# Seven products of blocks for the queries and the attention output of a macaron transformer block

## The chip, the cores and the metric

The kernel runs on one core of one Trainium2 chip. A core has five engines, each with its own queue of instructions that it works off in order: TensorE (matmuls; PE in the profile, its weight loads PEld), VectorE (DVE), ScalarE (ACT), GpSimd (POOL) and SyncE (SP), whose queue here issues every transfer between the memory outside the core and its own memory (SBUF). Matmuls write into PSUM, eight banks of 512 float32 per partition. Engines wait for each other by semaphores only. The metric is the device time of one execution in microseconds (us); the median of three runs counts.

## The reference

Eight sequences of 512 tokens with 512 features go through half a feed-forward, attention, and half a feed-forward again, everything in float32:

```python
x = x + 0.5 * ffn(layernorm(x))
x = x + attn(layernorm(x))
x = x + 0.5 * ffn(layernorm(x))

def ffn(x):
    h = silu(x @ w_gate) * (x @ w_up)            # 512 -> 2048
    return keep_two_largest_of_four(h) @ w_down  # by magnitude; 2048 -> 512

def attn(x):
    Q, K, V = x @ W_q, x @ W_k, x @ W_v          # 16 query heads, 4 key/value heads of 32
    Qr, Kr = rope(Q), rope(tile(K))              # rotation of neighbouring pairs
    weights = softmax(Qr @ Kr.T / sqrt(32))
    return (weights @ tile(V)) @ W_o
```

## The kernel before

The program is one long list of instructions, written by generators that a planner lets take turns. Sixteen feed-forwards ("blocks": eight sequences, two each, in a fixed order) are the main line. Everything else, the layernorm that gets a block's input ready and the eight attentions, are "sides": each is cut into steps, each step has a due place, counted in groups of matmuls of the main line (about 3.45 us each), and a step is written down when its due place has come and its inputs are there by the planner's own clock (`at`, three counters for TensorE, VectorE and ScalarE), or when it is three groups late. An attention runs over about 70 groups, and the next one begins where it ends.

VectorE's work stands in three waiting lists: `soon` (urgent), `later` (put off) and `for_later`. `fill`, called after each product, writes down as much of it as VectorE can finish by the time TensorE is done; last come the steps that zero two of four hidden values. `ensure` forces entries out.

The feed-forward already multiplies blocks with seven products in place of eight (the scheme of Strassen and Winograd): inputs and weights are cut into 2x2 quarters, sums of quarters are multiplied, and the products are put together. `woven` does it for gate and up: seven products of four matmuls, each 128x128 by 128x256, into three banks (x, v and z). Between the products VectorE and ScalarE copy or add a bank into its place. `product` (L561) does the same for the down projection with eight matmuls a product. The quarters of w_gu are loaded 16 ahead (`load_quarters`, L115 and L117), those of w_down three ahead. The sums of weights are made once: of w_gu in the first block by VectorE (`combine_gu`), of w_down by GpSimd (`combine_down`, two sides in the first block, into a big tile of the slot "wa").

An attention (`attention(b)`) has these steps:

- the layernorm (`layernorm_t`, tag "xa"): four row tiles of 128 tokens are loaded (L287), normalised and transposed into xT, with the features on the partitions; meanwhile the weights and the rotation tables cs are loaded (L798);
- five projections (`projected`, L809): K and four chunks of Q, each four matmuls of 128x128 by 128x512 into one of the same three banks. VectorE rotates each with four instructions: a shuffle of neighbours from the bank, a multiplication by the cosine from the bank, one by the sine, and a sum;
- V (L834): 16 matmuls 128 wide;
- scores and softmax per chunk of four heads, with matmuls on 32 rows each (L853, L886), maxima by VectorE, exponentials by ScalarE, sums by VectorE, weighted values (L902) and the division. The scores fill the four banks of the slot "sc";
- the output (L988): four products, each four matmuls 128x128 by 128x512, one per 128 tokens; VectorE adds each to the residual xt, and SP stores it (L996).

The slots: "p" holds two big tiles, used in turn by cs, xT, total and p; "wa" one, for wqkv and then wo; "xa" four row tiles, for xn and then xt. A tile is written only when all readers of the tile before it in the place are done.

The query projection is this:

```python
ps = Bank([P, S], "proj")
for k in range(ND):
    nc.tensor.matmul(out=ps.tile, lhsT=wa[:, k, col : col + P], rhs=xT[:, k, :], start=(k == 0), stop=(k == ND - 1))
```

Of the kernel before, what the change touches and what calls it, by code (L numbers as in the profile page):

```python
# [11 lines left out]
FP = mybir.dt.float32  # L12
# [6 lines left out]
P = 128  # L19
# [7 lines left out]
def macaron_block(  # L27
# [29 lines left out]
    wdp = ctx.enter_context(tc.tile_pool(name="wdp", bufs=3))  # L57
    sp = ctx.enter_context(tc.tile_pool(name="sp", bufs=1))
    wap = ctx.enter_context(tc.tile_pool(name="wap", bufs=1))
    qkvp = ctx.enter_context(tc.tile_pool(name="qkvp", bufs=1))  # L60
    pp = ctx.enter_context(tc.tile_pool(name="pp", bufs=2))
    xnp = ctx.enter_context(tc.tile_pool(name="xnp", bufs=4))
# [69 lines left out]
    z = const.tile([P, NT, N_KV, HD], BF, name="z")  # L132
    nc.vector.memset(z, 0.0)
    identb = const.tile([P, P], BF, name="identb")

# [13 lines left out]
    def multiplied(us, tiles=False):  # L151

        takes("pe", us + (SWITCH if tiles != tiled[0] else 0.0))
        tiled[0] = tiles
# [26 lines left out]
    def later(us, does, ready=None, queue=put_off):  # L181
        queue.append(Later(us, does, pe_heard() if ready is None else ready, queue))
        return queue[-1]
# [32 lines left out]
    w_slots = Slots(work, "w", 2)  # L216
    row_slots = Slots(cp, "row", 2)
    corner_slots = Slots(cp, "corner", 2)
    wa_slots = Slots(wap, "wa", 1)
    sc_slots = Slots(ps_sc, "sc", 1)  # L220
    acc_slots = Slots(ps_acc, "acc", 1)

# [56 lines left out]
    def layernorm_t(got, tag, src=None, xb=None):  # L279

        xn = []
        for t in range(NT):
            xn.append(xnp.tile([P, D], FP, tag=tag, name="xn"))
            if xb is None:
                nc.sync.dma_start(out=xn[t], in_=src[t * P : (t + 1) * P, :])  # L287
        mv = small.tile([P, NT, 2], FP, tag="mv", name="mv")
# [38 lines left out]
        def sums():  # L327

            xT = got["xT"]
            (b11, b12), (b21, b22) = ([xT[:, 2 * i : 2 * i + 2, j * HALF : (j + 1) * HALF] for j in range(2)] for i in range(2))  # L330
            got["sums"] = ts = tp.tile([P, 4, 2, HALF], FP, tag="ts", name="ts")
            got["made"] = [
                later(0.62, partial(nc.vector.tensor_tensor, ts[:, i], a, b, ALU.subtract), at["act"])
                for i, a, b in ((0, b12, b11), (1, b22, ts[:, 0]), (2, b22, b12), (3, b21, ts[:, 1]))
            ]

        if xb is None:
# [18 lines left out]
            for t in range(NT):  # L356
                turn(t)
                yield by_scalar if t < NT - 1 else now
            if tag == "xf":
                sums()  # L360
        else:

            function(AF.Sqrt)
# [16 lines left out]
    def fill(slack=HEARD):  # L380

        while True:
            steps = thin["next"]
            for queue in (urgent, put_off, for_later):
                if queue and queue[0].fits(slack):
                    queue[0].run()
                    break
            else:
                if not steps:
                    return  # L390
                ready = steps[1] if isinstance(steps[1], float) else steps[1]()
                if max(at["dve"], ready) + steps[0] > at["pe"] + slack:
                    return
                step()
# [101 lines left out]
    def combine_down(g):  # L496

        for c in range(2 * g, 2 * g + 2):
            raw = p_slots.tile([P, 4, D], FP, "raw")
            for r in range(4):  # L500
                nc.sync.dma_start(out=raw[:, r], in_=w_down[c][:, r])
                there = at["pe"] + 5.0
                yield now if r < 3 else lambda: there
            quarter = {f"{i + 1}{j + 1}": raw[:, i::2, j * HD2 : (j + 1) * HD2] for i in range(2) for j in range(2)}
            sums = wa_slots.tile([P, 6, 2, HD2], FP, "sums")

            for i, name in enumerate(SUMS):
                of = quarter[name[3:]] if name[3:] in quarter else sums[:, int(name[4:]) - 1]
                nc.gpsimd.tensor_tensor(sums[:, i], quarter[name[:2]], of, ALU.subtract)
                nc.sync.dma_start(out=combined[g, name][:, c % 2 * 2 : c % 2 * 2 + 2, :], in_=sums[:, i])  # L510
            yield now
        done_down.add(g)

# [266 lines left out]

    heads = [slice(kv * HD, (kv + 1) * HD) for kv in range(N_KV)]

    def attention(b):
        ensure(written[b, 0])
        wa = wa_slots.tile([P, ND, D + 2 * KV], FP, "wqkv")
        cs = p_slots.tile([P, 4, S], FP, "cs")
        loads = deque()
        for src, col in ((w_k, D), (w_v, D + KV)):
            loads.append((wa[:, :, col : col + KV], src.rearrange("(c p) n -> p c n", p=P)))
        for i in range(2):  # L790
            loads.append((cs[:, i], rope[i]))
        for k in range(ND):
            loads.append((wa[:, k, :D], w_q[k * P : (k + 1) * P, :]))
        got = {}
        for ready in layernorm_t(got, "xa", tokens[b][1]):
            if loads:
                dst, src = loads.popleft()
                nc.sync.dma_start(out=dst, in_=src)  # L798
            yield ready
        xT = got["xT"]  # L800
        qT = qkvp.tile([P, ND, S], FP, tag="qT", name="qT")
        kT = qkvp.tile([P, S], FP, tag="kT", name="kT")
        v = qkvp.tile([P, NT, KV], FP, tag="v", name="v")

        def projected(dst, col, scale):

            ps = Bank([P, S], "proj")
            for k in range(ND):
                nc.tensor.matmul(  # L809
                    out=ps.tile, lhsT=wa[:, k, col : col + P], rhs=xT[:, k, :], start=(k == 0), stop=(k == ND - 1)  # L810
                )
            multiplied(3.43)
            fill()
            sw = w_slots.tile([P, S], FP, "sw")
            soon(0.65, partial(nc.vector.stream_shuffle, sw, ps.tile, SWAP))
            read = soon(
                0.62, partial(nc.vector.scalar_tensor_tensor, dst, ps.tile, scale, cs[:, 0, :], ALU.mult, ALU.mult)
            )
            ps.free([read])
            soon(0.65, partial(nc.vector.scalar_tensor_tensor, sw, sw, scale, cs[:, 1, :], ALU.mult, ALU.mult))  # L820
            made = soon(0.65, partial(nc.vector.tensor_tensor, dst, dst, sw, ALU.add))
            return [p_slots.used(w_slots.used(made), 1)]

        of_k = projected(kT, D, 1.0)
        yield now
        of_q = []
        for c in range(ND):
            of_q.append(projected(qT[:, c, :], c * P, 1.0 / math.sqrt(HD)))
            yield now
        ensure(of_q[-1])  # L830
        vps = Bank([P, NT, KV], "vps")
        for t in range(NT):
            for k in range(ND):
                nc.tensor.matmul(  # L834
                    out=vps.tile[:, t, :],
                    lhsT=xT[:, k, t * P : (t + 1) * P],
                    rhs=wa[:, k, D + KV : D + 2 * KV],
                    start=(k == 0),
                    stop=(k == ND - 1),
                )  # L840
# [1 line left out]
        fill()  # L842
        nc.scalar.copy(v, vps.tile)
        vps.free(end=takes("act", 0.6, pe_heard()))
        wo = wa_slots.tile([P, ND, D + 2 * KV], FP, "wo")
        yield partial(when, of_k + of_q[0])

        def scores(c, t, nm):

# [82 lines left out]


        nm = maxima()
        ensure(of_k + of_q[0])
        for t in range(NT):
            found = scores(0, t, nm)
            nc.sync.dma_start(out=wo[:, t, :D], in_=w_o[t * P : (t + 1) * P, :])
            yield partial(when, found)
        pieces = in_pieces(nm)  # L940
        yield partial(when, pieces)
# [34 lines left out]
        waits(end)  # L976
        weighted(NT - 1, ops, p)
        out_of = divided(c, ops, sums)
        xts = []
        for t in range(NT):  # L980
            xts.append(xnp.tile([P, D], FP, tag="xa", name="xt"))
            nc.sync.dma_start(out=xts[t], in_=tokens[b][1][t * P : (t + 1) * P, :])
        yield partial(when, out_of)
        waits(ensure(out_of))
        for t, xt in enumerate(xts):
            y = Bank([P, D], "y")
            for k in range(ND):
                nc.tensor.matmul(  # L988
                    out=y.tile, lhsT=qT[:, k, t * P : (t + 1) * P], rhs=wo[:, k, :D], start=(k == 0), stop=(k == ND - 1)
                )  # L990
            multiplied(3.43)
            fill()

            def add(t=t, xt=xt, y=y):
                nc.vector.tensor_tensor(xt, y.tile, xt, ALU.add)
                nc.sync.dma_start(out=tokens[b][2][t * P : (t + 1) * P, :], in_=xt)  # L996

            made = [soon(0.62, add)]
            y.free(made)
            if t == NT - 1:  # L1000
                ensure(made)
            yield now

# [2 lines left out]
    WIDTH = 7 * NCH + 7 * NCH // 2  # L1008
    NORM = 5 + 2 * NT

    WEIGHTS = [0.5] * (NORM + ND + 2) + [0.7] * (NT + 1) + [0.9, 0.9] * NT
    WEIGHTS += ([0.9, 1.2] + [0.9, 0.9] * (NT - 1)) * (ND - 2) + [1.5] + [1.3] * (NT - 1) + [1.5] + [0.5] * NT
    ATTENTION = len(WEIGHTS)

    def place(b, i):
        return WIDTH * blocks.index((b, i))


    sides = [(10, 19, 10, partial(combine_down, 0), None, None), (22, 34, 10, partial(combine_down, 1), None, None)]
    for b, i in blocks[1:]:  # L1020
        stage = partial(layernorm_t, normed[b, i], "xf", tokens[b][2 * i])
        sides.append((place(b, i) - 15, place(b, i) - 2, NORM, stage, ("attention", b) if i else None, None))
# [106 lines left out]
```

## Time and profile before

| what | us |
|---|---|
| median of 3 runs | 3211.94 (3211.62 to 3216.32) |
| the profiled execution, whole | 3210.11 |
| its span, first to last instruction | 3208.2 |
| TensorE busy | 3176.9 |
| VectorE busy | 2189.8 |
| ScalarE busy | 1195.8 |
| GpSimd busy | 507.2 |
| of TensorE's time along the chain that ended last: projections L809 | 4.3% |
| output products L988 | 3.4% |

Busy time is the time in which an engine has at least one instruction at work. Matmuls overlap at their ends, and a float32 matmul stands as two records; so the length of a matmul row is longer than its share of the time, and the distance from one start to the next is the price. A wait is idle time of an engine with the instruction that ended it. The engines' shares are averages over stages, and only an engine that others wait for costs time.

### The profile page before, as it was taken

The numbers are of one execution on the slowest core, as the hardware profiler recorded it, in microseconds if no ns is written. First come the engines' busy times: TensorE is split into PE (matmuls) and PEld (weight loads), VectorE is DVE, ScalarE is ACT, GpSimd is POOL, SyncE is SP. The second block draws the span as 40 slices with busy tenths as digits, with TensorE's granted clock in tenths as the row PEclk, the third lists the DMA queues.
The fourth block names the chain that finished last, engine by engine and source line by source line (L and its number), as shares of the span: only waits on it lengthen the run. The fifth ranks groups of instructions, "written<-read, shape, count | busy, mean of one in ns | idle before, by whom it ended". The sixth has DMA issues, their size and how long they took to land.

```text
span 3208.2 us, 43276 instructions
## 1 busy us (share of the span) xinstructions
PE 3176.9 (99%) x15880; PEld 2322.4 (72%) x15880; DVE 2189.8 (68%) x4718; ACT 1195.8 (37%) x1683; POOL 507.2 (16%) x822
## 2 busy tenths in 40 slices
PE   8999999999999999999999999999999999999999
PEld 6887767767677677766776677766776677666886
DVE  7756876587657785678657865777567765776554
ACT  2222454145522553245314542255324441454220
POOL 2322102110021111101211102111120121111110
PEclk9999999999999999999999999999999999999999
DMA  7763344434443436334444344443633444434441
GB/s 236 240 216 99 122 158 144 142 128 126 156 158 126 132 119 210 96 121 152 145 143 131 122 153 159 133 132 112 210 99 119 161 141 142 131 122 154 154 165 53
DMA packets 263731, 462.15 MB, mean 144 GB/s; under 512 B 25952, under 2 KB 81760, under 8 KB 263264
## 3 DMA queue, kind: packets, MB, share of 16 engines
q1 hardware_dynamic: 263520, 459.38, 44.2%
q8 instruction: 127, 2.08, 0.3%
q14 instruction: 84, 0.69, 0.1%
HBM read 421.53 MB, written 37.75 MB: 143 GB/s over the span
## 4 chain that ended last, share of the span: by engine, by line
PE 96%; DVE 2%; DMA 1%; ACT 1%; POOL 0%; issue 0%; SPq 0%; POOLq 0%; DVEq 0%
PE x L636 27%; PE v L636 13%; PE x L561 13%; PE z L636 7%; PE v L561 6%; PE proj L809 4%; PE st L886 4%; PE sc L853 4%; PE ops L902 4%; PE y L988 3%; PE z L561 3%; PE tr L263 1%; PE gu L611 1%; PE den L918 1%; PE vps L834 1%; PE st L891 1%
## 5 line engine op out<-in xcount | busy, mean ns | idle before, releaser
L636 PE MATMUL x<-ts,w 128*128 128x256 f32 x3000 | 717.3, 382 | 1.4 <-DVE corner L650 1.4
L636 PEld LDWEIGHTS x<-ts,w 128*128 128x128 f32 x3000 | 561.7, 190 | 137.9 <-issue 44.3
L452 POOL TENSOR_TENSOR e<-h 128x512 f32<-128x512 f32 x62 | 79.3, 1279 | 2232.5 <-DVE h L446 1892.9
L165 DVE TENSOR_REDUCE nm<-sc 128x1 f32<-128x512 f32 x512 | 321.1, 683 | 95.3 <-PE sc L853 94.0
L561 PE MATMUL x<-wd,h 128*128 128x256 f32 x1488 | 339.9, 382 | 0.0
L165 DVE TENSOR_TENSOR total<-total,p 128x512 f32<-128x512 f32 x384 | 273.8, 749 | 81.1 <-ACT p L894 81.1
L561 PEld LDWEIGHTS x<-wd,h 128*128 128x128 f32 x1488 | 280.2, 190 | 62.5 <-issue 19.3
L894 ACT ACTIVATE p<-st 128x2048 f32<-128x2048 f32 x96 | 179.7, 1872 | 291.1 <-PE st L891 279.8
L255 ACT ACT_TABLE_LOAD x215 | 275.8, 1283 | 4.5 <-PEq L1118 0.7
L243 ACT COPY row<-x 128x512 f32<-128x512 f32 x207 | 121.2, 585 | 393.0 <-PE x L636 392.9
L685 ACT ACTIVATE h<-x 128x256 f32<-128x256 f32 x125 | 47.6, 381 | 555.2 <-PE x L636 543.3
L636 PE MATMUL v<-ts,w 128*128 128x256 f32 x1000 | 239.0, 382 | 2.4 <-ACT xT L324 2.4
L636 PE MATMUL x<-xT,w 128*128 128x256 f32 x1000 | 239.4, 382 | 1.8 <-ACT xT L324 1.8
L636 PE MATMUL v<-xT,w 128*128 128x256 f32 x1000 | 238.5, 382 | 1.5 <-DVE corner L245 1.5
L636 PE MATMUL z<-xT,w 128*128 128x256 f32 x1000 | 238.9, 382 | 0.0
L561 PE MATMUL v<-wd,e 128*128 128x256 f32 x992 | 228.2, 382 | 7.1 <-POOL e L452 4.0
L561 PEld LDWEIGHTS v<-wd,e 128*128 128x128 f32 x992 | 186.2, 190 | 52.6 <-issue 13.3
L636 PEld LDWEIGHTS x<-xT,w 128*128 128x128 f32 x1000 | 186.9, 190 | 49.2 <-issue 20.4
L636 PEld LDWEIGHTS v<-ts,w 128*128 128x128 f32 x1000 | 187.3, 190 | 46.2 <-issue 16.2
L636 PEld LDWEIGHTS z<-xT,w 128*128 128x128 f32 x1000 | 187.1, 190 | 45.6 <-issue 19.3
L636 PEld LDWEIGHTS v<-xT,w 128*128 128x128 f32 x1000 | 187.7, 190 | 42.8 <-issue 10.1
L407 ACT ACTIVATE a<-h 128x1024 f32<-128x1024 f32 x128 | 134.9, 1054 | 186.0 <-DVE m L425 106.8
(115 smaller groups left out, 4448.8 us busy)
## 6 DMA issues: line engine op xcount, KB each, us to landing
w<-gu SPq DMA_DIRECT2D x472, 256.0 KB, 3.4
w<-in_w_gu SPq DMA_DIRECT2D x394, 256.0 KB, 3.4
wd<-wd SPq DMA_DIRECT2D x124, 512.0 KB, 5.4
wd<-in_w_down SPq DMA_DIRECT2D x186, 256.0 KB, 3.6
x<-x SPq DMA_DIRECT2D x64, 256.0 KB, 2.6
xn<-x SPq DMA_DIRECT2D x64, 256.0 KB, 5.0
x<-in_x SPq DMA_DIRECT2D x32, 256.0 KB, 3.7
gu<-w SPq DMA_DIRECT2D x32, 256.0 KB, 2.9
```

What stands on the lines that cost most here:

```text
L165: self.does()
L243: nc.scalar.copy(dst, src)
L255: nc.scalar.activation(dummy[:, 1:2], dummy[:, 0:1], f)
L407: nc.scalar.activation(a, h[:, :, half * HALF : (half + 1) * HALF], AF.Abs)
L561: nc.tensor.matmul(out=y.tile[:, t, :], lhsT=part[:, t * P : (t + 1) * P], rhs=operands[i][:, n, :], start=(first and t == 0 and n == 0), ...
L636: nc.tensor.matmul(out=bank.tile[:, m, :], lhsT=lhs[:, m, k, :], rhs=rhs[:, k, :], start=(first and m == 0 and k == 0), stop=(k == 1), ski ...
L809: nc.tensor.matmul(out=ps.tile, lhsT=wa[:, k, col : col + P], rhs=xT[:, k, :], start=(k == 0), stop=(k == ND - 1))
L853: nc.tensor.matmul(out=sc[:, kv, :], lhsT=qT[rows, c, t * P : (t + 1) * P], rhs=kT[rows, :], start=True, stop=True)
L886: nc.tensor.matmul(out=st[:, kv, :], lhsT=kT[rows, t * P : (t + 1) * P], rhs=qT[rows, c, :], start=True, stop=False)
L894: nc.scalar.activation(p, st, AF.Exp)
L902: nc.tensor.matmul(out=ops[rows, :], lhsT=v[:, t, rows], rhs=p[:, kv, :], start=(t == 0), stop=(t == NT - 1))
L988: nc.tensor.matmul(out=y.tile, lhsT=qT[:, k, t * P : (t + 1) * P], rhs=wo[:, k, :D], start=(k == 0), stop=(k == ND - 1))
```

## The change

The four query projections become seven products of four matmuls 128x128 by 128x256, and so do the four output products. They go to three of the four banks of the scores' slot (bank order 0, 1, 0, 1, 0, 2, 0), one product a step, with other work between. The factors:

- queries: sums of quarters of w_q, made once, by sums of quarters of the tokens, made per attention by VectorE in a tile of the "p" slot; the first three products are copied to their places in qT, the next three added there and rotated, and the last is rotated from the bank;
- output: quarters and sums of the heads' outputs (four sums by VectorE per attention) by quarters and sums of w_o; all seven products are added to the residual.

The sums of w_q and w_o are made by VectorE in the second block (`combine_qo`) and stored to memory outside. All quarters are loaded through four small tiles ("waq"), each next one when a product is written down. The rotation tables are loaded once (`load_cs`). The sums of w_down, by GpSimd as before, also use the four small tiles. xn and xt of an attention become one tile each of four rows. The attention has more steps, so their spacing changes. w_q and w_o are laid out by quarters before the launch. The diff, cut:

```diff
+    waq = ctx.enter_context(tc.tile_pool(name="waq", bufs=4))
...
+    cs = const.tile([P, 2, S], FP, name="cs")
...
-    wa_slots = Slots(wap, "wa", 1)
...
-        xn = []
+        if tag == "xf":
+            xn = [xnp.tile([P, D], FP, tag=tag, name="xn") for _ in range(NT)]
+        else:
+            xa = xnp.tile([P, NT, D], FP, tag=tag, name="xn", bufs=1)
+            xn = [xa[:, t, :] for t in range(NT)]
...
+            if tag == "xf":
+                got["sums"] = ts = tp.tile([P, 4, 2, HALF], FP, tag="ts", name="ts")
+            else:
+                got["sums"] = ts = p_slots.tile([P, 4, 2, HALF], FP, "ts")
             got["made"] = [
-                later(0.62, partial(nc.vector.tensor_tensor, ts[:, i], a, b, ALU.subtract), at["act"])
+                (later if tag == "xf" else soon)(
+                    0.62, partial(nc.vector.tensor_tensor, ts[:, i], a, b, ALU.subtract), at["act"]
+                )
...
-            sums = wa_slots.tile([P, 6, 2, HD2], FP, "sums")
+            sums = []
+            for name in SUMS:
+                sums.append(waq.tile([P, 2, HD2], FP, tag="waq", name="sum"))
...
+    def combine_qo():
+        for which, how in (("q", Q_SUMS), ("o", O_SUMS)):
+            both = [p_slots.tile([P, 4, 2, HALF], FP, "both") for _ in range(2)]
+            w = [both[q // 4][:, q % 4] for q in range(8)]
+            for q in range(4):
+                nc.sync.dma_start(out=w[q].rearrange("p a b -> p (a b)"), in_=flat(qo_raw[which][q]))
+                there = at["pe"] + 5.0
+                yield now if q < 3 else lambda: there
+            for to, a, b, op in how:
+                made = later(0.65, partial(nc.vector.tensor_tensor, w[to], w[a], w[b], op), queue=for_later)
+            yield partial(when, [made])
+            ensure([made])
+            nc.sync.dma_start(out=qo_sums[which], in_=both[1])
+            yield now
+
+    def load_qo(which, q):
+        w = waq.tile([P, 4 * P], FP, tag="waq", name="waq")
+        src = flat(qo_raw[which][q]) if q <= Q21 else flat(qo_sums[which][:, q - S1])
+        nc.sync.dma_start(out=w, in_=src)
+        return w
...
+        def seven(lhs, rhs, take):
+            sc = sc_slots.tile([P, N_KV, 2, HALF], FP, "seven")
+            waits(sc_slots.ready)
+            order = 0, 1, 0, 1, 0, 2, 0
+            taken = {bank: [] for bank in order}
+            for i, bank in enumerate(order):
+                waits(ensure(taken[bank]))
+                w = weights.popleft()
+                for m in range(2):
+                    for k in range(2):
+                        nc.tensor.matmul(
+                            out=sc[:, bank, m, :],
+                            lhsT=lhs(w, i, m, k),
+                            rhs=rhs(w, i, k),
+                            start=(i in (0, 1, 5) and m == 0 and k == 0),
+                            stop=(k == 1),
+                            skip_group_check=True,
+                        )
+                multiplied(1.73)
+                load_next()
+                fill()
+                taken[bank] = take(i, sc[:, bank])
+                for entry in taken[bank]:
+                    sc_slots.used(entry)
+                yield partial(when, taken[order[i + 1]] if i < 6 else [])
...
-        for c in range(ND):
-            of_q.append(projected(qT[:, c, :], c * P, 1.0 / math.sqrt(HD)))
-            yield now
...
+        def take_query(i, bank):
...
+            if i < 3:
+                return [Done(copied((left, corner, right)[i], bank))]
+            if i == 6:
+                return rotate(below, 0, bank)
+            to, j = ((right, 1), (corner, 1), (left, 0))[i - 3]
+            entry = soon(0.62, partial(nc.vector.tensor_tensor, to, bank, to, ALU.add))
+            rotate(to, j)
+            return [entry]
+
+        yield from seven(
+            lambda w, i, m, k: w[:, (2 * m + k) * P : (2 * m + k + 1) * P],
+            lambda w, i, k: tokens_of[i][:, k, :],
+            take_query,
+        )
+        yield partial(when, of_k + of_q)
...
-        xts = []
+        xt = xnp.tile([P, NT, D], FP, tag="xa", name="xt", bufs=1)
         for t in range(NT):
-            xts.append(xnp.tile([P, D], FP, tag="xa", name="xt"))
-            nc.sync.dma_start(out=xts[t], in_=tokens[b][1][t * P : (t + 1) * P, :])
+            nc.sync.dma_start(out=xt[:, t, :], in_=tokens[b][1][t * P : (t + 1) * P, :])
...
+        combined_heads = p_slots.tile([P, 4, 2, HALF], FP, "sums")
...
+        def take_output(i, bank):
+            def add(to):
+                nc.vector.tensor_tensor(to, bank, to, ALU.add)
+                if i >= 5:
+                    for t in (0, 1) if i == 5 else (2, 3):
+                        nc.sync.dma_start(out=tokens[b][2][t * P : (t + 1) * P, :], in_=xt[:, t, :])
+
+            made = [soon(0.62, partial(add, (left, corner, right, right, corner, left, below)[i]))]
+            if i == 6:
+                ensure(made)
+            return made
...
-    WEIGHTS = [0.5] * (NORM + ND + 2) + [0.7] * (NT + 1) + [0.9, 0.9] * NT
-    WEIGHTS += ([0.9, 1.2] + [0.9, 0.9] * (NT - 1)) * (ND - 2) + [1.5] + [1.3] * (NT - 1) + [1.5] + [0.5] * NT
+    WEIGHTS = [0.5] * (NORM + 2 + 7 + 1) + [0.7] * (NT + 1) + [0.9, 0.9] * NT
+    WEIGHTS += ([0.9, 1.2] + [0.9, 0.9] * (NT - 1)) * (ND - 2) + [1.5] + [1.3] * (NT - 1) + [1.5, 0.7] + [0.5] * 7
...
-    sides = [(10, 19, 10, partial(combine_down, 0), None, None), (22, 34, 10, partial(combine_down, 1), None, None)]
+    sides = [(10, 19, 10, partial(combine_down, 0), None, None), (22, 34, 10, partial(combine_down, 1), None, None), (36, 40, 2, load_cs, None, None), (43, 56, 12, combine_qo, None, None)]
```

## The prediction

> **What bounds the kernel now.** First the page's busy times, for the engine that could be the bound:
>
> ```profile
> PE 3176.9 (99%) x15880; PEld 2322.4 (72%) x15880; DVE 2189.8 (68%) x4718; ACT 1195.8 (37%) x1683; POOL 507.2 (16%) x822
> ...
> PEclk9999999999999999999999999999999999999999
> ```
>
> TensorE is busy 99% of 3208.2 us at the full clock. A busy share can hide waits inside, so next come the same times split at 110 us (columns: length, then PE, PEld, DVE, ACT, POOL busy, clock, DMA share):
>
> ```profile
> 0.00:110.00 110.00, 94.64 (x383) 73.05 (x384) 88.75 (x173) 27.77 (x50) 29.73 (x26) 1.00 0.75 247
> 110.00:3208.20 3098.20, 3082.26 (x15499) 2249.34 (x15497) 2101.09 (x4546) 1168.03 (x1633) 477.44 (x796) 1.00 0.43 140
> ```
>
> And the longest waits of TensorE (line, who ended the wait, us in total, times, longest):
>
> ```profile
> PE tr L263 <- DVE xn L373: 7.4, 3, 6.4
> PE v L561 <- POOL e L452: 4.0, 4, 1.5
> PE st L886 <- DVE nm L165: 3.1, 2, 1.5
> PE v L561 <- DMA wd<-in_w_down: 2.9, 1, 2.9
> ```
>
> Of 31.3 us in which TensorE is idle, 15.4 lie in the first 110 us, where this change moves no matmul; 15.9 are spread over the other 3098. Once under way, the kernel is one stream of matmuls, and its time is the length of that stream. What is left to read is the price of each piece, from the order of time (start, length, then the group):
>
> ```profile
> 241.71 3.60 PE L809 MATMUL proj<-xT,wqkv 128*128 128x512 f32 x8
> 245.14 1.89 PE L636 MATMUL x<-ts,w 128*128 128x256 f32 x8
> 246.87 1.89 PE L636 MATMUL z<-xT,w 128*128 128x256 f32 x8
> ```
>
> The lengths overlap, so prices are differences of starts: a projection of four matmuls, 512 columns wide, takes 245.14 - 241.71 = 3.43 us; a product of four matmuls 256 wide takes 1.73 (the next one 1.72). I use 3.43 and 1.725.
>
> **The change, part by part.**
>
> *The matmuls.* Per attention the queries lose four projections (4 x 3.43 = 13.72 us) and get seven products of the shape of L636 (7 x 1.725 = 12.08); the output projection likewise. That is 1.64 us for each of 16 stages: -26.3 us, and it lies on the bound. The K projection, V, scores and feed-forward keep their matmul counts. Built, the changed kernel has as many changes between 32-row and full matmuls as this one (528 both), so what these cost cancels. One rule of the Trainium skill speaks against this: "TensorE: Matmul & The Clock Gate", section Back-to-back issue gap, says that in a stream of weight loads and matmuls a narrow one costs more per column, 81 ns at 128 columns against 131 at 512. A line between these gives about 98 at 256 (an estimate from that page), so 28 narrow matmuls would cost 28 x 98 / (16 x 131) = 1.31 times the 16 wide ones: +4.2 us a stage, +67 in all, 3277 us. The row above has the same shape and type in this kernel, and two halves cost 2 x 1.725 = 3.45 against 3.43. The row decides.
>
> *VectorE.* Each query stage gets four sums of tokens and three additions from banks (before, the rotation read its bank directly; the four rotations stay, at the same four instructions each). Each output stage gets four sums of heads and seven additions in place of four. So seven more instructions a stage, at 0.69 us (128x512 rows of L165 and L650, 686 and 691 ns): 4.8 us a stage, 77 in all. Three copies per query stage go to ScalarE at 0.59. Twenty table loads on ScalarE fall away; it is 37% busy, so I count nothing. What hides the 4.8 us is idle VectorE in these very stages; windows from the first projection to the end of V, summed over the eight attentions,
>
> ```profile
> sum 265.70, PE 265.70 PEld 177.31 DVE 178.44 ACT 27.69 POOL 23.54; mean PE 33.21 PEld 22.16 DVE 22.30 ACT 3.46 POOL 2.94
> ```
>
> and the output stages:
>
> ```profile
> sum 182.70, PE 181.91 PEld 112.01 DVE 98.83 ACT 28.62 POOL 25.11; mean PE 22.74 PEld 14.00 DVE 12.35 ACT 3.58 POOL 3.14
> ```
>
> VectorE idles (265.7 - 178.4) / 8 = 10.9 us per query stage and (182.7 - 98.8) / 8 = 10.5 per output stage, twice what is added. If that cover failed, up to 77 us would show. The planner now gives more steps to the projections, so the scores and weights between get some 4 feed-forward groups less (43 against 47, about 14 us of 244). VectorE is 73% busy there, 1434.6 of 1956 us; about 74 us per attention are its own maxima and sums ((321.1 + 273.8) / 8), the other 105 are feed-forward. Without 14 of some 200 us of feed-forward this becomes (74 + 98) / 230 = 75%. I count nothing.
>
> *Waits of the new products.* Four of the seven share one bank and two another, and each waits until VectorE or ScalarE has read the product before it there. In the built order at least three other products (5.2 us) stand between; the feed-forward does the same behind one product of 1.73 us (L636, z between two x), and in 3208 us waited 1.5 and 1.4 us for such a reader. Zero. The scores now need all queries, not one chunk: at least 5.2 us of feed-forward stand between the last query product and the first scores, and its rotation takes 2.8 (727 + 674 + 682 + 691 ns). Zero. The sums of tokens take the place of cs in the two p slots, and the sums of heads make a fifth use; each new owner comes after the last reader of the old one in the order anyway. Zero.
>
> *Shared port.* "SBUF — State Buffer", section SBUF: two separate sides, says that a VectorE instruction with two inputs in SBUF and a GpSimd instruction exclude each other for its whole length. The trace agrees: the same sum of 128x256 takes 418 ns in one place, 540 on the mean in another, once 1.49 us. The change adds 64 such sums (of tokens and heads), eight of weights, and 24 rotations that read the queries from SBUF and no longer from the bank: 96 x 0.69 = 66 us of lock. GpSimd is busy 16% of the time, so some 10 us of delay is spread over both engines. TensorE waits for GpSimd for 4.0 us now. Between 0 and 10; I take 1.
>
> *Transfers and SP's queue.* Per attention, k and v (2 loads), cs (2), q (4) and wo (4) become k and v (2) and 14 quarters: 16 issues for 12, 0.4 us each, 1 MB more of about 58 per attention. A quarter's load waits in SP's queue until the product that had its place is done. So do the feed-forward's own loads (L115, L117) behind it, and those are 16 quarters (27 us) ahead of TensorE. Zero. At the boundary between attentions there is a later start: the tokens and residual are one tile now, so the first xn load waits for the landing of all four stores of xt. Before, with TensorE done at 548.3, SP issued the last store at 549.19 and the first xn at 550.58, which lands 5.2 us later, 7.5 after TensorE. Now the last store goes out some 2.5 us after TensorE and lands 3.5 later, the first xn 5.2 after that: some 11.5. The statistics are then late; behind them VectorE has a sum that the feed-forward needs at 562.36, 14 us after. That leaves 2.5 us. Seven boundaries, 0 to 2 us each; I take 1 us in all.
>
> *Once.* In block two, w_q and w_o are loaded (2 MB), eight sums of 0.78 us (row of L705) are made, and 2 MB are stored. The store waits on SP for VectorE, with the feed-forward's loads behind it; the 27 us ahead cover it. The last four sums run as one piece, 3.1 us, with the next addition behind them: 0 to 3 us, I take 1. GpSimd's sums of w_down get four small tiles for one big one, and less to wait for: zero, or a gain of up to the 2.9 us that TensorE waits for wd.
>
> **Sum.** Profiled execution: 3208.2 of span and 1.9 around it, 3210.1. With -26.3 for matmuls and +3 for waits: 3186.8. The median of the runs lies 1.8 above the profiled one, so 3188.5.
>
> **The rivals.**
>
> *R1, waits eat part of it.* The boundaries cost 1 us each (7), the shared port 4, the once-only part 3: 14 in place of 3, and 3199.5; with 2 us at each boundary 3206.5. For it: the 2.5 us of margin is small, and VectorE works in order. Against: each of the waits is below what the kernel rides out now.
>
> *R2, slower.* VectorE in the query stage: the four rotations (2.8 us each) follow each other at 3.45 us of TensorE, and feed-forward additions queue behind them. If TensorE stalled in each of 16 stages for more than 26.3 / 16 = 1.64 us, the gain would be gone; if all 4.8 us came through it would be 3208.2 + 1.9 + 1.8 - 26.3 + 77 = 3263. For it: with the feed-forward's work VectorE is locally full. Against: the rotations are pulled in only when VectorE is free in the plan, rotations already come every 5.16 us at 601 to 625 us, and there TensorE waits for nothing.
>
> *R3, no change.* The narrow product costs more beside these operands than in the feed-forward: at 1.96 us instead of 1.725 the gain is zero (13.72 / 7). The 3500 matmuls of L636 show one price whatever their operands, so this is unlikely.
>
> **How the numbers follow.** Forecast 0.72, with its own range 3180 to 3196: the waits after 110 us could shrink by 8 us or grow by 10. R1 0.14, R2 0.08, R3 0.06. A measurement of this kernel can tell about 0.2% from no change, 6.4 us, so 3205.5 to 3218.4 is the same. Of R1, 0.01 ends there. Faster 0.72 + 0.13 = 0.85, same 0.07, slower 0.08. The range, 3179 to 3206, takes in the forecast and R1 and leaves out R2 and R3.
>
> **What would show it.** In the profile after: the products start 1.72 to 1.73 us apart and TensorE's busy time is near 3150.6; its idle time stays at 28 to 40 us, with no wait on the bank of the new products above 2 us in all; VectorE is busy near 2273 (77 and the eight sums more). The prediction is wrong if TensorE's idle time grows by more than 15 us (then see who is waited for at the boundaries and in the query stages), or if the product's price isn't 1.725.

## The result, and the profile after

The changed kernel takes 3198.39 us (median of 6 runs, 3195.94 to 3201.11), and the kernel before, run beside it, 3214.89: the ratio is 0.995, with a 95% interval of 0.9937 to 0.9963. That is 16.5 us less, where 23.4 were forecast (3211.94 - 3188.5); the median lies inside the range that was given, 3179 to 3206. The profiled execution took 3196.95 us, of which 3195.2 are its span.

The page's busy times and clock, after:

```profile
PE 3152.2 (99%) x16264; PEld 2391.6 (75%) x16264; DVE 2278.1 (71%) x4840; ACT 1177.4 (37%) x1665; POOL 524.5 (16%) x822
...
PEclk9999999999999999999999999999999999999999
```

TensorE's busy time fell from 3176.9 to 3152.2, by 24.7 us, with 3150.6 forecast. VectorE's rose to 2278.1, with 2273 forecast. What was not forecast is TensorE's idle time: 3195.2 - 3152.2 = 43.0 us, where it was 31.3, 34 was expected, and 28 to 40 was given as the sign of being right. The split at 110 us shows that all of the growth lies behind it (14.4 us idle before, 28.6 after; it was 15.4 and 15.9):

```profile
0.00:110.00 110.00, 95.56 (x388) 74.01 (x389) 87.71 (x173) 27.77 (x50) 30.34 (x26) 1.00 0.76 248
110.00:3195.20 3085.20, 3056.62 (x15878) 2317.64 (x15876) 2190.37 (x4669) 1149.66 (x1615) 494.13 (x796) 1.00 0.46 145
```

The longest waits of TensorE, after, say for whom it waits:

```profile
PE v L569 <- POOL e L460: 13.0, 8, 2.4
PE st L1002 <- DVE nm L167: 8.9, 7, 1.9
PE tr L264 <- DVE xn L381: 7.3, 3, 6.3
```

The waits for GpSimd's sums of hidden values, e, grew from 4.0 to 13.0 us, those of the scores that feed the exponentials (st) for VectorE's maxima, nm, from 3.1 to 8.9. Neither is a wait of the new products (seven), which stand nowhere among TensorE's waits. One of them takes 614.18 - 612.45 = 1.73 us in the order of time, after:

```profile
610.72 1.89 PE L644 MATMUL x<-ts,w 128*128 128x256 f32 x8
612.45 1.89 PE L889 MATMUL seven<-xT,waq 128*128 128x256 f32 x8
614.18 1.89 PE L644 MATMUL z<-xT,w 128*128 128x256 f32 x8
```

Windows summed over the eight attentions, after, say where (sum of lengths, then PE, PEld, DVE, ACT and POOL busy). First the query stages, from the K projection to the last product:

```profile
sum 290.90, PE 290.90 PEld 247.36 DVE 187.59 ACT 52.53 POOL 33.17; mean PE 36.36 PEld 30.92 DVE 23.45 ACT 6.57 POOL 4.15
```

then the output stages:

```profile
sum 213.00, PE 213.00 PEld 187.49 DVE 120.22 ACT 37.75 POOL 25.53; mean PE 26.62 PEld 23.44 DVE 15.03 ACT 4.72 POOL 3.19
```

then the stage of scores and weights between them:

```profile
sum 1908.00, PE 1887.30 PEld 1310.20 DVE 1477.97 ACT 877.48 POOL 270.91; mean PE 235.91 PEld 163.77 DVE 184.75 ACT 109.69 POOL 33.86
```

and that stage, before:

```profile
sum 1956.00, PE 1947.80 PEld 1369.86 DVE 1434.61 ACT 925.85 POOL 260.76; mean PE 243.47 PEld 171.23 DVE 179.33 ACT 115.73 POOL 32.60
```

TensorE has no gap in either stage that was rebuilt. It idles 20.7 us in the stage between, whose own instructions the change does not alter, and idled 8.2 there before: 12.5 more. VectorE is busy 1478.0 / 1908.0 = 77.5% there, up from 1434.6 / 1956.0 = 73.3%. (The first window of before leaves out 14 us behind V; with them in, its length is 1974.5 us, and the idle time and the share are the same.)

How one of these waits comes about can be seen at 475 us. VectorE in order of time, after (start, length, instruction):

```profile
472.79 1.43 DVE L454 SCALAR_TENSOR_TENSOR h<-m,h 128x256 f32<-128x256 bf16 x4
474.13 0.41 DVE L167 TENSOR_TENSOR h<-h,x 128x256 f32<-128x256 f32 x1
474.46 0.69 DVE L583 SCALAR_TENSOR_TENSOR x<-x 128x512 f32<-128x512 f32 x1
475.06 2.78 DVE L167 TENSOR_TENSOR total<-total,p 128x512 f32<-128x512 f32 x2
```

and GpSimd in the same window:

```profile
474.35 1.26 POOL L460 TENSOR_TENSOR e<-h 128x512 f32<-128x512 f32 x1 [63.94 <-DVE h L454]
475.69 1.59 POOL L461 TENSOR_TENSOR e<-e,h 128x512 f32<-128x512 f32 x1
477.37 1.60 POOL L462 TENSOR_TENSOR e<-h,e 128x512 f32<-128x512 f32 x1
```

VectorE ends the zeroing of hidden values (L454) at 474.2, when the down products have already begun. GpSimd starts the first sum e at 474.35, and the second down product, which reads it, has waited 1.58 us when it goes on at 475.67. At the same time two of VectorE's sums total take 2.78 us, where one takes 684 ns without GpSimd's sums (e7 below), and two of GpSimd's three take 1.59 and 1.60 us where the first took 1.26: each holds up the other.

### The profile page after: what moved, and what is told of

It reads as the page before. It is cut to its first block, busy times and chain, and to the rows that moved or that the text cites. A ratio compares the mean times of both kernels' runs of the same rounds, so it can differ in the third digit from the quotient of the medians.

```text
span 3195.2 us, 44283 instructions
## 1 busy us (share of the span) xinstructions
PE 3152.2 (99%) x16264; PEld 2391.6 (75%) x16264; DVE 2278.1 (71%) x4840; ACT 1177.4 (37%) x1665; POOL 524.5 (16%) x822
## 4 chain that ended last, share of the span: by engine, by line
PE 93%; DVE 5%; DMA 1%; POOL 0%; ACT 0%; issue 0%; SPq 0%; DVEq 0%; POOLq 0%; ACTq 0%
PE x L644 26%; PE v L644 13%; PE x L569 12%; PE z L644 7%; PE v L569 6%; PE seven L889 6%; PE st L1002 4%; PE sc L969 4%; PE ops L1018 4%; PE z L569 3%; PE tr L264 1%; PE gu L619 1%; DVE total L167 1%; PE vps L919 1%; PE den L1034 1%; PE st L1007 1%
## 5 line engine op out<-in xcount | busy, mean ns | idle before, releaser
L167 DVE TENSOR_TENSOR total<-total,p 128x512 f32<-128x512 f32 x384 | 286.4, 781 | 68.9 <-ACT p L1010 68.6
L644 PEld LDWEIGHTS v<-xT,w 128*128 128x128 f32 x1000 | 186.8, 190 | 47.1 <-issue 7.5
```

The source lines that it names most:

```text
L167: self.does()
L644: nc.tensor.matmul(out=bank.tile[:, m, :], lhsT=lhs[:, m, k, :], rhs=rhs[:, k, :], start=(first and m == 0 and k == 0), stop=(k == 1), ski ...
```

## The experiments

Idle time is TensorE's, span minus busy time, in the profiled execution; times are medians, with the ratio to the kernel before in the same session. That kernel's own median lay between 3211.58 and 3214.89 from session to session, so kernels of different sessions are compared by their ratios. "z second" is another order of the down products, shown with e5; "no e" leaves out GpSimd's sums of hidden values.

| kernel | us | ratio, 95% | idle | waits for e | for maxima |
|---|---|---|---|---|---|
| before | 3211.94 | 1 | 31.3 | 4.0 | 3.1 |
| after | 3198.39 | 0.9950 (0.9937 to 0.9963) | 43.0 | 13.0 | 8.9 |
| e1 after, wide spacing | 3213.01 | 1.0000 (0.9991 to 1.0008) | 51.2 | 18.3 | 6.6 |
| e2 after, dense spacing | 3197.04 | 0.9952 (0.9936 to 0.9969) | 42.3 | 7.8 | 6.1 |
| e3 before, dense spacing | 3221.66 | 1.0031 (1.0022 to 1.0041) | 40.2 | 9.9 | 3.5 |
| e4 after, no new sums | 3199.21 | 0.9958 (0.9943 to 0.9973) | 44.7 | 13.2 | 8.9 |
| e5 after, z second | 3186.91 | 0.9921 (0.9908 to 0.9935) | 35.2 | 2.3 | 10.3 |
| e6 before, z second | 3213.76 | 1.0006 (0.9998 to 1.0014) | 31.7 | 1.4 | 3.1 |
| e7 after, no e | 3173.61 (one) | | 23.8 | 0 | 0 |
| e8 before, no e | 3202.02 (one) | | 24.9 | 0 | 0 |
| e9 after, z second, wide | 3194.28 | 0.9934 (0.9917 to 0.9951) | 38.7 | 4.4 | 6.7 |
| e10 after, z second, dense | 3194.51 | 0.9939 (0.9924 to 0.9954) | 43.1 | 1.9 | 8.9 |
| e11 before, z second, dense | 3214.55 | 1.0003 (0.9993 to 1.0012) | 33.5 | 2.3 | 4.9 |
| e12 after, z second, not in the first seven | 3184.02 | 0.9905 (0.9888 to 0.9921) | 33.8 | 2.3 | 10.3 |

**Is it the spacing, or the work?** The change gives the attention more steps within the same 70 groups of feed-forward, so its scores and weights stand closer together: by the planner, 46.8 groups on the mean from first scores to first output product, and 51 before. Theory: this squeeze makes VectorE late. Rivals: the added instructions do, wherever they stand, or the port they share with GpSimd. Three kernels change the spacing alone, one takes work away. e1 widens the stage between to 51 groups:

```diff
-    WEIGHTS = [0.5] * (NORM + 2 + 7 + 1) + ...  [1.5, 0.7] + [0.5] * 7
+    WEIGHTS = [0.4] * (NORM + 2 + 7 + 1) + ...  [1.5, 0.3] + [0.2] * 7
```

> The changed kernel with other step weights alone: 0.4 for the layernorm and query steps and 0.3 and 0.2 for the output steps, so that 51 groups of feed-forward stand between the first scores and the first output product, as before the change (46.8 in the changed kernel). Squeeze theory (TensorE's idle time of 43.0 us against 31.3 comes from scores and weights that stand closer together, so that VectorE's maxima and sums push the zeroing of hidden values back): idle time 30 to 35 us, 3186 to 3191. Rival, amount of work (VectorE's 122 more instructions push everything back wherever they stand): idle 40 to 45 us, 3196 to 3200. Rival, shared port: as the amount theory.

e2 squeezes it to 43.4 groups, with 0.65 and 1.1, 0.8 in these places:

> The changed kernel squeezed further by step weights alone: 0.65 for the layernorm and query steps, 1.1 and 0.8 for the output, 43.4 groups between first scores and first output product in place of 46.8. Squeeze theory: about as much again as the first 4.2 groups, idle time 50 to 60 us, 3204 to 3212. Amount of work and shared port: idle 41 to 46 us, about 3198.

e3 squeezes the kernel before to 47.1:

```diff
-    WEIGHTS = [0.5] * (NORM + ND + 2) + ...  [1.5] + [0.5] * NT
+    WEIGHTS = [0.6] * (NORM + ND + 2) + ...  [1.5] + [1.1] * NT
```

> The kernel before, squeezed by step weights alone (0.6 for the layernorm and projection steps, 1.1 for the output steps): 47.1 groups between first scores and first output product in place of 51. Same work on every engine. Squeeze theory: idle time grows from 31.3 to 40 to 44 us, 3221 to 3226 beside about 3213 of before. Amount of work and shared port: idle stays at 31 to 33, no change.

e4 leaves the 64 new sums out of the changed kernel:

```diff
-        tokens_of = b11, ts[:, 0], ts[:, 1], b22, ts[:, 2], b21, ts[:, 3]
+        tokens_of = b11, b12, b22, b22, b12, b21, b21
...
-        heads_of = a11, *(combined_heads[:, i] for i in (0, 1, 3, 2)), a12, a22
+        heads_of = a11, a21, a22, a12, a21, a12, a22
```

> The changed kernel without the 64 sums of tokens and heads by VectorE: the products take plain quarters in their place, so the products are of other numbers. The same matmuls, steps and spacing (46.6 groups between). Squeeze theory: most waits stay, idle 38 to 43 us, 3194 to 3198. Amount of work, or the port through these two-input sums: idle 31 to 36 us, 3187 to 3192.

e4 takes away 46 of the 88 us by which VectorE's busy time had grown (2232.1 are left), and the two waits are the same to 0.2 us. So these sums are not behind them; the other additions and copies were not taken away. The waits of e4:

```profile
PE v L572 <- POOL e L463: 13.2, 8, 2.4
PE st L1004 <- DVE nm L167: 8.9, 7, 1.9
```

e3 is as the squeeze theory says: with no other work at all the kernel before loses 10 us, and most of that, 5.9 us, to e:

```profile
PE v L561 <- POOL e L452: 9.9, 7, 2.0
...
PE st L886 <- DVE nm L165: 3.3, 3, 1.5
```

But the theory falls as a rule of more and less. e2, squeezed further, has fewer waits for e, not more; its time and idle time are those that the rivals expected. e1, as wide as the kernel before, is the worst of all, which neither theory had: 18.3 us for e, one wait of 5.9, and other waits besides. First the waits for e of e1, then those of e2:

```profile
PE v L569 <- POOL e L460: 18.3, 9, 5.9
```

```profile
PE v L569 <- POOL e L460: 7.8, 8, 2.0
```

So the spacing moves these waits, by several microseconds either way, but the number of groups doesn't say which way. The kernel before has a spacing at which they are small, and none of the other spacings tried matches it.

**Is it the sums e?** What the waits have in common is GpSimd. e5 and e6 keep spacing and work, and move only the readers of e back. The down products are reordered so that the first reader of e starts 6.9 us after the first product and no longer 3.45:

```diff
     PRODUCTS = (
         ("11", "11", "x", (0, 0)),
-        (0, "12-11", "v", (1, 1)),
+        ("12", "21", "z", (0, 0)),
         (1, "22-T1", "x", (0, 1)),
-        (2, "22", "v", (0, 1)),
+        (0, "12-11", "v", (1, 1)),
         ("21", "22-12", "x", (1, 1)),
-        ("12", "21", "z", (0, 0)),
+        (2, "22", "v", (0, 1)),
         ("22", "21-T2", "x", (1, 0)),
```

> The changed kernel with the seven down products in another order: the product of plain hidden values into bank z comes second, and the first product of GpSimd's sums e third, 6.9 us after the first product and no longer 3.45. Nothing else moves; the spacing is the same. Theory (late zeroing: with more of VectorE's urgent work per feed-forward group the zeroing of hidden values is done only just before the down products, and GpSimd's sums behind it are late): TensorE's 13.0 us of waits for e and the 1.6 us of lost clock go, idle 29 to 32 us, 3181 to 3185. Rival (the waits for e stand for VectorE being late in general): the waits turn up at the next reader of VectorE's work, idle 38 to 44 us, 3192 to 3199.

> The kernel before with the same new order of the down products. Late zeroing: it has only 4.0 us of waits for e to lose, idle 26 to 29 us, 3206 to 3209 beside about 3212; the difference between the two kernels in this order is then the matmul term, 24 to 27 us. Rival: no change, and the difference stays at 13 to 16 us.

By the ratios the changed kernel gains some 9 us on its old order (0.9950 to 0.9921), and the one before nothing. The difference between the two in this order is 3213.76 - 3186.91 = 26.9 us, as large as the whole matmul term. The waits of e5:

```profile
PE st L1002 <- DVE nm L167: 10.3, 8, 1.9
PE tr L264 <- DVE xn L381: 7.4, 3, 6.4
PE v L569 <- DMA wd<-wd: 3.1, 1, 3.1
PE x L569 <- POOL e L461: 2.3, 2, 2.0
```

The waits for e are gone but for 2.3 us, 2.0 of them in the first block, and did not turn up at another reader of the same work. GpSimd is no earlier: in the case at 475 us its first sum starts 474.35 - 469.61 = 4.74 us after the first down product, and in e5 again 473.42 - 468.68 = 4.74. Only the reader is later, and it no longer waits:

```profile
468.68 3.62 PE L569 MATMUL x<-wd,h 128*128 128x256 f32 x16
...
475.58 3.69 PE L569 MATMUL x<-wd,e 128*128 128x256 f32 x16
```

The idle time, 35.2, is 3 to 6 above what was expected, and the time 2 above its range: the waits for maxima stayed, and in the first block 3.1 us came in for w_down's sums from memory (wd). The kernel before has such a wait in the old order too (2.9 us), and e4 as well (3.1), so it does not take the new order. The kernel before did not gain the 3 us that were expected: its waits for e fell from 4.0 to 1.4, but 2.0 us came in for ScalarE's copies of corner, and TensorE's busy time rose from 3176.9 to 3180.3, with a lowered clock in two of its windows of 40 us (0.96 at 80 and at 2120 us; the last section has more on this).

**What stands behind the maxima?** e7 and e8 leave GpSimd's sums of hidden values out of both kernels:

```diff
-            if sums is not None:
-                (h11, h21), (_, h22) = ([h[:, i::2, :HALF], h[:, i::2, HALF:]] for i in range(2))
-                if half == 1:
-                    nc.gpsimd.tensor_tensor(sums[:, 0], h21, h22, ALU.add)
-                    ...
...
-                            part = e[:, side, n % 2, :]
+                            part = h[:, 2 * (n % 2) + side % 2, :HALF]
```

> The changed kernel without GpSimd's four sums of hidden values per pair of chunks (248 instructions of 1.3 us): the products take plain quarters, so the products are of other numbers. No wait for e is left, and no GpSimd lock on VectorE. Shared port behind the waits for maxima (8.9 us): these fall to under 4 us and the mean of the sums total<-total,p from 781 to about 685 ns; idle 20 to 26 us. VectorE simply full there: the waits for maxima stay at 6 to 10, idle 28 to 32.

> The kernel before without the same sums of hidden values, which are left out here too. No wait for e; idle 25 to 28 us, or 22 to 25 if the lock stands behind its waits for maxima of 3.1 us. Span of this minus span of the changed kernel without e: 24 to 27 us if all that the change lost was behind GpSimd, 18 to 21 if the waits for maxima stay.

Each ran once. No wait for maxima is left in either, and the two kernels idle alike, 23.8 and 24.9 us. Their spans differ by 3200.2 - 3171.7 = 28.5 us, where 24 to 27 were expected if all of the loss was behind GpSimd. The page's busy times of e7:

```profile
PE 3147.9 (99%) x16264; PEld 2392.5 (75%) x16264; DVE 2206.5 (70%) x4840; ACT 1177.7 (37%) x1665; POOL 184.8 (6%) x574
```

The group of the sums total of after (busy us and mean ns of one behind the first bar):

```profile
L167 DVE TENSOR_TENSOR total<-total,p 128x512 f32<-128x512 f32 x384 | 286.4, 781 | 68.9 <-ACT p L1010 68.6
```

of before:

```profile
L165 DVE TENSOR_TENSOR total<-total,p 128x512 f32<-128x512 f32 x384 | 273.8, 749 | 81.1 <-ACT p L894 81.1
```

and of e7:

```profile
L167 DVE TENSOR_TENSOR total<-total,p 128x512 f32<-128x512 f32 x384 | 249.2, 684 | 71.0 <-ACT p L1001 71.0
```

VectorE has the same 4840 instructions and is busy 2278.1 - 2206.5 = 71.6 us less: that is what GpSimd's sums cost it in the changed kernel. In the kernel before it is 2189.8 - 2129.0 = 60.8. The 10.8 between them stand in the sums total, which lose 286.4 - 249.2 = 37.2 us after and 273.8 - 248.9 = 24.9 before (684 ns each in e8, as in e7); the other instructions lose about as much in both. So what the change lost in waits hangs on GpSimd's sums: by their lateness (e5), and, for the maxima, by the time that VectorE loses to them. The second rests on one execution of each kernel.

**Does spacing still matter then?** e9, e10 and e11 combine the new order with the three spacings:

> The changed kernel with z second and the wide spacing (51 groups between first scores and first output product) that alone had cost time: 3213, idle 51.2 us, of which 18.3 for e, and some 10 us of lost clock behind its long waits. If the loss of that spacing was the same waits for e, with the clock lost behind them: idle 32 to 38 us, 3184 to 3192. If spacing costs in its own way (late sides, forced steps): idle above 42, 3196 to 3206.

> The changed kernel with z second and the dense spacing (43.4 groups), which alone came to 3197 with 7.8 us of waits for e. Waits for e gone: idle 33 to 37 us, 3185 to 3190, so that the spacing no longer matters. Squeeze theory (VectorE too full there): 3194 or more.

> The kernel before with z second and the denser spacing that alone had cost it 10 us (idle 40.2, of which 9.9 for e). If that loss was the waits for e: idle 30 to 34 us, 3210 to 3214, the same as the kernel before. If it was VectorE being full: 3218 to 3224.

e11 settles e3: the squeezed kernel before gets back what the squeeze cost it (3214.55, no change against before), so its loss was the waits for e. e9 recovers 21 of the 25 us by which e1 stood above e5 (by the ratios), and no more: at that spacing transposes wait 4.3 us for VectorE, 3.3 of them at once, and scores 5.0 for maxima. e10 missed its forecast: its waits for e fell to 1.9, but idle time is 43.1, as before the new order, with 4.3 us of waits of the new products for VectorE's additions into qT, which read their bank, 2.5 for ScalarE's copy of the transposed maxima (mT) and 8.9 for maxima:

```profile
PE st L1002 <- DVE nm L167: 8.9, 7, 1.9
...
PE seven L889 <- DVE qT L167: 4.3, 2, 2.6
...
PE den L1034 <- ACT mT L993: 2.5, 2, 1.6
```

So each spacing has costs of its own. Which arrangement of the maxima and sums against the zeroing is good was not separated further.

**A better kernel.** e12 keeps the old order in the program's first seven down products, where e5 waited for weights:

```diff
+            order = FIRST_PRODUCTS if (b, final) == blocks[0] and g == 0 else PRODUCTS
```

> The changed kernel with z second everywhere but in the first seven down products of the program, where the order is that of before. With z second throughout, TensorE waited there for weights (3.1 us) and for e (2.0), and the clock fell behind it (1.6 us lost); in the old order it waited 2.85 for late zeroing and no clock was lost. If these are losses of that place alone: idle 32 to 34 us, 3182 to 3186. If the start only shifts its waits: as with z second throughout, 3186 to 3188.

It takes 3184.02 us, 0.9905 of before, against 0.9921 for e5; the intervals overlap, so e5 and e12 can't be told apart. (The profile of e12 is that of its slowest run, 3189.03 us, with 2.0 us of waits for e and 2.0 for the zeroing in that place.) Both are faster than both given kernels.

## Why the prediction was right, and where it was off

*The matmuls: right.* The price of a product beside its new operands is 1.73 us, and the narrow matmuls cost no more per column, so the +67 us that the prediction weighed against the change did not come. The term of -26.3 measures -27.4 in TensorE's busy time of e8 and e7 (3175.3 - 3147.9), where no wait for e or maxima is left, and -26.9 between the medians of e6 and e5. R3 is out.

*VectorE in the rebuilt stages: right.* VectorE's busy time grew by 88.3 us, where 83 were forecast (77 and the eight sums once); 77.5 of them are instructions (e7 against e8) and the rest time lost to GpSimd's sums. TensorE has no gap in 290.9 and 213.0 us, and e4 shows that taking 64 of the sums away brings nothing. But not all of the new work ran in these stages (below). R2 is out.

*Waits of the new products, transfers, boundaries, the second block: right at or near zero.* None of them appears among TensorE's waits. At the first boundary the last output product ended at 551.9, the first xn load went out at 556.1, and the statistics ran from 563.3, before the addition behind them at 566.0.

*The stage between: the step that failed.* It said "this becomes (74 + 98) / 230 = 75%. I count nothing." Both the sum and the use made of it were wrong. The stage became 8.3 us shorter per attention and not 14 (1974.5 and 1908.0 us over eight), and VectorE's work in it did not fall to 172 us but came to 1478.0 / 8 = 184.7. The sum left out what spills over from the rebuilt stages: 73 of VectorE's instructions in these windows, 51 us by their lengths, are the tail of the queries' rotations (41) and the sums of heads (32), and before there were none. With them the share is 77.5%, but the waits don't follow from them: e4 leaves the sums of heads out and waits as much, and in each of the eight stages the first wait for e or maxima comes 80 us or more behind the last query product.

The larger mistake is to read a cost from a share at all. The zeroing is the last in VectorE's lists, GpSimd's sums follow it, and a down product follows those after 3.45 us; the planner keeps no clock for GpSimd. Before, this chain cost TensorE 4.0 us, and after, 13.0; e5 takes the wait away by a later reader alone. What makes the zeroing itself later in the changed kernel, rather than in some other arrangement, stays open: other spacings moved the wait to 18.3 and 7.8 us (e1, e2), and to 9.9 in the kernel before (e3), by no rule that was found.

*The shared port: right in kind, mis-sized.* "Between 0 and 10; I take 1" looked at the new sums and rotations alone. The new sums matter little (e4). What counts is the old sums total against GpSimd's, with 71.6 us of VectorE's time lost in place of 60.8, and the waits for maxima behind it: 5.8 us more than before, and none left without GpSimd's sums (e7).

*The sum.* 3 us of waits were allowed for. The idle time grew by 11.7: +9.0 for e, +5.8 for maxima, and -2.9 for a wait for wd in the first block. The last is no gain to count on: in e4, which has the same first block, it stands at 3.1. With 1.6 us of TensorE's busy time above the forecast, as much as was lost to a lowered clock at 365 us (below), the profiled execution is 10.2 us above its forecast of 3186.8. The range held because it was wide enough for R1, whose 3199.5 is nearer to the 3198.39 measured than the forecast's 3188.5. It is R1 in size and not in place: the boundaries, where R1 put half of its loss, cost nothing.

## What to carry to other kernels

Where one engine is busy 99%, shorten its stream, and price the new pieces by a row of the same shape in the same trace: that part of the forecast held to 1 us in 26. The rest is decided by chains over slower engines at the end of everybody's lists, which a busy share of 75% does not show. Follow the instructions with the lowest priority to the one that the bound engine waits for, and see by how little it is in time today. Here a reader of such a chain that was moved behind other work (e5) was a better cure than any other spacing (e1, e2, e9, e10). And when a stage is rebuilt, add to its neighbour the work that will run over into it.

## What the runs showed of the hardware

A wait of TensorE can cost more than its length. After, the second down product at 361.8 us waits 2.37 us for e, and then its remaining twelve records of matmuls take 4.54 us where they take 2.86 behind a wait of 1.58:

```profile
365.19 4.54 PE L569 MATMUL v<-wd,e 128*128 128x256 f32 x12 [2.37 <-POOL e L460]
...
475.67 2.86 PE L569 MATMUL v<-wd,e 128*128 128x256 f32 x12 [1.58 <-POOL e L460]
```

The windows there show why. The granted clock (the figure after the five engines) falls to 0.75, 0.50 and 0.90 in three windows of 2 us: (0.25 + 0.50 + 0.10) x 2 = 1.7 us are lost, which is what some 3.4 us at half clock lose.

```profile
365.00:367.00 2.00, 1.81 (x6) 1.55 (x7) 0.00 (x0) 0.00 (x0) 1.84 (x3) 0.75 0.15 52
367.00:369.00 2.00, 2.00 (x6) 1.53 (x6) 0.00 (x0) 0.00 (x0) 2.00 (x2) 0.50 0.00 0
369.00:371.00 2.00, 2.00 (x10) 1.72 (x9) 1.23 (x3) 0.00 (x0) 0.05 (x1) 0.90 0.21 37
```

It does not follow every such wait. The kernel before waited 2.95 us at 105 us, and its windows there show the full clock:

```profile
108.47 3.85 PE L561 MATMUL v<-wd,e 128*128 128x256 f32 x16 [2.95 <-DMA wd<-in_w_down]
```

In the same place e4 waits 3.07 us, and the same sixteen records take 5.38. In e1 two waits for e of the same 1.90 us are followed by 4.54 us for twelve records (1916.65) and by 2.86 (876.57). TensorE's busy time of e1 is 3162.1 us for the same matmuls, 11.5 above the forecast 3150.6, and its windows of 40 us show a lowered clock in seven of them, 12 us in sum. The Trainium skill ("TensorE: Matmul & The Clock Gate", section What's actually happening) has the two clock states, and a window of 3.4 us that runs free of the work. That this window decides which wait is hit would fit these pairs, but no run here shows it. Its table asks for an idle window of about 3.4 us, and here waits of 2.37 and of 1.90 us were enough.
